# Splitting GpSimd's multiply by the reciprocals in the last attention block into two halves, one unit apart

## The chip, the cores and the metric

The kernel runs on one core of a Trainium2 chip, in one launch for all four batch images. The metric is the device time of one execution in microseconds, as the median of several runs; lower is better. The engines are named as in the profile: PE (TensorE, matrix products), PEld (its weight loads), DVE (VectorE), ACT (ScalarE), POOL (GpSimd) and SP (SyncE, which only issues transfers here).

## The reference

Layer 0 is self-attention over the 4096 positions of each 256-channel image; layer 1 normalizes, clusters, and applies an MLP and a pointwise layer to its output. The change is in layer 0:

```python
q = jnp.einsum('oc,bcn->bno', wq, xf) + bq
k = jnp.einsum('oc,bcn->bon', wk, xf) + bk[None, :, None]
attn = jax.nn.softmax(jnp.einsum('bnd,bdm->bnm', q, k), axis=-1)
v = jnp.einsum('oc,bcn->bon', wv, xf) + bv[None, :, None]
out = jnp.einsum('bcn,bmn->bcm', v, attn).reshape(B, Cc, H, W)
return gamma[0] * out + x
```

The kernel divides by the softmax denominator last: it sums the exponentials of a query's row, multiplies V by the raw exponentials, scales that by gamma, and multiplies the result by the reciprocal of the sum. That last multiply is what the change touches.

## The kernel before, in words

*Tiles and units.* An image has 8 blocks of 512 queries (`NBLK`), and each block goes over 8 groups of 512 keys (`GRP`). One group of one block is a unit, `u`; there are 64 a batch, and `nb, g = divmod(u, GRP)`. Block 7 (units 56 to 63) is the last block; in it `more` is false, since no further block has to be scored.

*One unit.* The scores of a unit lie in a tile `s` as four quarters (`B11`, `B12`, `B21`, `B22`: two halves of the keys by two halves of the queries). `exps(u + 1)`, called at the start of unit `u`, subtracts the row maximum on DVE (L655) and takes the exponentials on ACT (L659 to L661). `factors(u + 1)`, called in the middle of unit `u`, makes the sums that a seven-product scheme for 2 x 2 blocks needs: one on DVE (L678, `t13`), then four on GpSimd through `plus` (L664): `s[B12]`, `t4`, and the two running sums of the denominators, `acc` ("one" and "both"). `weigh` (L716 to L740) then issues the seven products of exponentials and V on TensorE, in four parts; the order of the products is `ORDER` = (1, 5), (2, 3), (7, 6), (4,), and in unit 63 `LAST` = (1, 5), (7, 6), (2, 3), (4,). Product 6 reads GpSimd's `s[B12]` (in the trace "av<-s,sum" behind "av<-t,sum"), product 4 reads its `t4` ("av<-t,v" in fourth place).

*What is left of the block ahead.* While block `nb` runs, block `nb - 1` is finished: `combined` (L771 to L780) puts the seven products' banks together on GpSimd, two pieces a unit in units g = 0 to 2; `total` (L782 to L795) makes the reciprocals of its denominators in a tile `rdens`; `leave(nb - 1)` (L801 to L806) multiplies the tile `t` (128 partitions, four rows of 256) by them on GpSimd, in place; `sent(nb - 1)` (L808 to L812) writes `t` to a DRAM tile `att`, as two transfers on SP's queue, one for rows 0 and 3 and one for rows 1 and 2. In block 7 `leave` stands at g = 3 (unit 59) ahead of the fourth part of `weigh`, and `sent` at g = 4 (unit 60).

*What comes after.* At unit 62 (`units - 2`) `back_one` (L832 to L835) issues on GpSimd's queue a transfer that adds block 6 of `att` to the input image `x` in SBUF; it waits until `att` is written. The `factors` of unit 63 stand behind it on GpSimd. DVE then takes block 6's statistics from that sum (`seen`, L850, and `pooled`, L855). In unit 63 the last denominators are summed on DVE (L684, L685, L748, L750), and behind the loop block 7 is finished by DVE (L779, L780, L1120, L846), while TensorE is given fills: projections of the next batch (L443), or in the last batch one block of the batch ahead (L1554). Then the cluster stage begins (L307 on). Behind `sent` SP's queue holds, from `tail` (L965 to L980): the mix weights (L167), the next image (L109) and the MLP weights (L242, L243).

*The order of work* is written out by hand: each engine runs its instructions in the order in which the program issues them, and waits on semaphores for the others. Nothing is moved by a scheduler.

Of the kernel before, what the change touches and what calls it, by code (L numbers as in the profile page):

```python
# [11 lines left out]
ALU = mybir.AluOpType  # L12
# [48 lines left out]
def attention_then_cluster_block(  # L61
# [17 lines left out]
    nc = tc.nc  # L79
# [51 lines left out]
    x00, part = load_x(0, 0, 2)  # L131
# [206 lines left out]
    def attention(b, xs, ys):  # L338
# [5 lines left out]
        qs, ks, slots, mxs, accs, tops, rdens, ts = {}, {}, {}, {}, {}, {}, {}, {}  # L344
# [452 lines left out]
        def over(nb):  # L797
            rden = rdens[nb].rearrange("p (h n) -> p h n", h=2).unsqueeze(2)
            return rden.to_broadcast([P, 2, 2, QW])

        def leave(nb):  # L801

            t = ts[nb].rearrange("p (h k) n -> p h k n", h=2)
            nc.gpsimd.tensor_tensor(t, t, over(nb), ALU.mult)
            if "t" not in own:
                own["t"] = dram.tile([NBLK // 2, P, KC, 2, NB], F32, tag="t", name=f"att_{b}")  # L806

        def sent(nb):  # L808

            t = ts.pop(nb)  # L810
            for k in range(KC):
                nc.sync.dma_start(out=own["t"][nb // 2][:, k, nb % 2], in_=rows_of(t, k))  # L812
# [126 lines left out]
        for u in range(units):  # L939
            three = u in (1, 3, 7, 9)  # L940
            for part in (0, 1, 3) if three else (0, 2) if u else (1, 3):
                if todo:
                    p, h = todo.pop(0)
# [14 lines left out]
        def weighting(next_x, fill, early, begin):  # L958

            mb, av, den, peak, quarters = None, None, iter(()), iter(()), iter(())  # L960

            views = {units - 6 + i: i for i in range(6)}
            shifts = {units - 10: 0, units - 9: 1, units - 8: 2, units - 7: 3}

            def tail(u):  # L965


                for at_u, f in (
                    (units - 12, lambda: load(0)),
                    (units - 10, lambda: (load(2), back(0))),  # L970
                    (units - 9, lambda: (load(3), back(1))),
                    (units - 8, lambda: back(2)),
                    (units - 5, lambda: (next_x(), next_x())),
                    (units - 4, lambda: (load_mix(b), next_x())),
                    (units - 4, lambda: b == B - 1 and load_mlp(b)),
                    (units - 3, lambda: (next_x(), begin())),
                    (units - 2, lambda: b < B - 1 and load_mlp(b)),
                ):
                    if u == at_u:
                        f()  # L980

            for u in range(units):
                nb, g = divmod(u, GRP)
                more = nb + 1 < NBLK
                ripe = more and nb and g == 5

                short = nb == 0 and g == 6
                if g == 0:
                    av = [
                        pool.tile([P, NB], F32, tag=tag, name=f"av{c}_{b}_{nb}")  # L990
                        for c, (pool, tag) in enumerate(
                            ((ps_a, "a0"), (ps_a, "a1"), (ps_m, "m"), (ps_m, "m"))
                        )
                    ]
                maxima = due(u, 0)
                if more and nb and g == GRP - 2:
                    next(peak)
                    if u == units - 10:
                        load(1)
                    sent(nb - 1)  # L1000
                if g == GRP - 1 and more:
                    gather(nb)
                if g + 1 < GRP or more:
                    exps(u + 1)
                for f in maxima:
                    f()
                if nb < 2 or g == 6:
                    caught(1)


                when = 1 if nb > 1 else 3
                if nb and g == when:
                    den = total(nb - 1)
                    next(den)
                elif nb and g == when + 1:
                    next(den)
                elif ripe:
                    peak = highest(nb + 1)
                    next(peak)
                if early and nb > 1:  # L1020
                    early.pop(0)()
                if u == 4:
                    spare()
                if u in views:
                    pooled(views[u])
                    seen(views[u], (0,))
                if g == GRP - 1 and not more:
                    gather(nb)
                weigh(u, av, 0)
                if short:  # L1030
                    two = ps_s.tile([P, 2, NB], F32, tag="s", name=f"tt_{b}_{nb + 1}")
                    tp = turned_over(nb + 1, two[:, 0].rearrange("p (j n) -> p j n", j=4))
                for f in due(u, 1):
                    f()
                weigh(u, av, 1)
                if short:
                    dgs["dg"] = across(nb + 1, "w2", tp)
                if u == units - 2:
                    back_one(NBLK - 2)
                maxima = due(u, 2)  # L1040
                if g == GRP - 1:
                    evict(nb, av, 0)
                    evict(nb, av, 2 if more else 1)
                if g + 1 < GRP or more:
                    factors(u + 1)
                if more and nb and g == GRP - 2:
                    known(mb)
                for f in maxima:
                    f()
                if ripe:  # L1050
                    next(peak)
                    mb = next(peak)
                if (u, 0) not in at or (u, 1) in at:
                    caught(1)
                if u in views:
                    seen(views[u], (1,))
                weigh(u, av, 2)
                if g == GRP - 1:
                    evict(nb, av, 1 if more else 2)
                if short:  # L1060
                    spread(nb + 1, dgs["dg"])
                for f in due(u, 3):
                    f()
                if nb and g == when:
                    next(den)
                elif nb and g == (5 if nb == 1 else 4 if more else 3):
                    leave(nb - 1)
                elif nb and g == 4 and not more:
                    sent(nb - 1)
                weigh(u, av, 3)  # L1070
                if g == 3 and nb + 2 < NBLK:
                    q_block(nb + 2)
                if g == GRP - 1:
                    evict(nb, av, 3)
                    quarters = combined(nb, nc.gpsimd if more else nc.vector)
                elif nb and g < 3:
                    for _ in range(2):
                        next(quarters)
                if u in shifts:
                    shift(shifts[u])  # L1080
                tail(u)

            nb = NBLK - 1
            for _ in range(4):
                next(quarters)
            if b == B - 1:
                for _ in turn_mlp():
                    pass
            table(AF.Sqrt)
            ends = b == B - 1  # L1090
            fill(1 if ends else 2)
            two = ps_s.tile([P, 2, NB], F32, tag="s", name=f"den_{b}_{nb}")
            den, inv = two[:, 0], two[:, 1]
            for j in range(4):
                nc.tensor.matmul(
                    den[j * D : (j + 1) * D, :P],
                    ones[:, :D],
                    rdens[nb][:, j * P : (j + 1) * P],
                    start=True,
                    stop=True,  # L1100
                )
            fill(1)
            rec = work.tile([P, P], F32, tag="top", bufs=1, name=f"rec_{b}_{nb}")
            nc.vector.reciprocal(rec, den[:, :P])
            for _ in quarters:
                pass
            seen(nb - 1)
            pooled(nb - 1)
            for j in range(4):
                nc.tensor.matmul(  # L1110
                    inv[:, j * P : (j + 1) * P],
                    ident[:, j * D : j * D + 1].to_broadcast([P, P]),
                    rec,
                    start=True,
                    stop=True,
                )
            nc.scalar.copy(rdens[nb], inv)
            fill(6 if ends else 7)
            t = ts[nb].rearrange("p (h k) n -> p h k n", h=2)
            nc.vector.tensor_tensor(t, t, over(nb), ALU.mult)  # L1120
            add_one(nb)
            seen(nb)
            return stats, cells, lambda: pooled(nb)
# [1042 lines left out]
```

## Time and profile before

| | us |
|---|---|
| median of 3 runs | 3116.73 |
| runs | 3112.5, 3117.52, 3116.73 |
| profiled execution | 3112.69 |
| its span, first to last instruction | 3110.9 |
| busy: PE / DVE / POOL / ACT | 3042.2 / 2501.5 / 2327.7 / 1779.4 |
| L804, the multiply: 28 instructions | 66.2 in all, 2.363 each |
| L664, GpSimd's acc, 128x512: 408 instructions | 541.4 in all, 1.347 each |
| PE waiting for POOL's s (L664) at L734, 9 times | 3.5 in all |
| granted TensorE clock | 0.998 of full speed |

How to read it: an engine's busy time counts its instructions; a share of the whole span is an average over stages with different limits, so what a change in one block is worth has to be read in that block. In the lines of the timeline the columns are start in us from the beginning of the span, duration in us, engine, line, operation, output and inputs, shapes, and, in brackets, idle time of the engine just ahead of the instruction and what ended it. "x2" is two instructions merged into one row. There are 28 L804 in four batches, one for each of the first seven blocks; the last of each batch, in block 7, starts at 501.16, 1269.19, 2036.64 and 2779.43 us.

### The profile page before, as it was taken

How to read it: one execution, taken by the hardware profiler on the slowest of the kernel's cores; microseconds unless marked ns; L12 is line 12 of the kernel's file. 1: busy time of each engine (PE TensorE's matmuls, PEld its weight loads, DVE VectorE, ACT ScalarE, POOL GpSimd, SP SyncE). 2: the span in 40 equal slices, each digit the busy share in tenths (PEclk: the TensorE clock that was granted, in tenths of full speed). 3: DMA queues.
4: the chain of work that ended last, by engine and by line, in shares of the span. 5: the costliest groups of instructions: out<-in, count | busy, mean ns of one | idle time of the engine just before them, and what ended most of it. 6: DMA issues, size and time to landing. Idle time of an engine off the chain costs nothing.

```text
span 3110.9 us, 41355 instructions
## 1 busy us (share of the span) xinstructions
PE 3042.2 (98%) x14210; PEld 2488.0 (80%) x14210; DVE 2501.5 (80%) x3548; ACT 1779.4 (57%) x2817; POOL 2327.7 (75%) x2243
## 2 busy tenths in 40 slices
PE   8999999999999999999999999999999999999999
PEld 5788887788688888878868888887877888885886
DVE  4998888777798888877779888877768988887675
ACT  5666664544566666454456666645456666655444
POOL 6888887477588888648758888965766988894563
PEclk9999999999999999999999999999999999999999
DMA  5112226100112113510011222441011212150000
GB/s 175 45 58 65 62 84 176 58 18 28 52 45 68 55 62 108 159 48 28 18 58 45 69 62 65 117 147 35 28 41 48 59 54 68 55 154 2 13 21 28
DMA packets 105570, 200.40 MB, mean 64 GB/s; under 512 B 14880, under 2 KB 30864, under 8 KB 103824
## 3 DMA queue, kind: packets, MB, share of 16 engines
q1 hardware_dynamic: 100464, 178.66, 18.0%
q0 software_dynamic: 4256, 18.90, 2.9%
q8 instruction: 113, 1.85, 0.2%
q14 instruction: 97, 0.79, 0.1%
q10 hardware_dynamic: 640, 0.20, 0.0%
HBM read 147.01 MB, written 48.34 MB: 63 GB/s over the span
## 4 chain that ended last, share of the span: by engine, by line
PE 74%; DVE 9%; POOL 8%; issue 3%; ACT 3%; DMA 2%; SPq 1%; POOLq 0%; ACTq 0%; DVEq 0%
PE av L734 34%; PE mo L1776 10%; PE sc L489 7%; PE hq L1859 5%; PE hp L1859 3%; PE hr L1859 3%; PE fv L1334 3%; POOL acc L664 3%; DVE s L655 2%; POOL t L664 2%; DVE top L513 2%; PE vp L443 1%; POOL s L664 1%; PE mo L1760 1%; DMA w<-in_w 1%
## 5 line engine op out<-in xcount | busy, mean ns | idle before, releaser
L502 ACT COPY s<-sc 128x1024 f32<-128x1024 f32 x512 | 515.1, 1012 | 427.5 <-PE sc L489 419.0
L655 DVE TENSOR_TENSOR s<-s,hold 128x1024 f32<-128x1024 f32 x512 | 598.4, 1209 | 10.7 <-ACT hold L638 5.5
L664 POOL TENSOR_TENSOR acc<-acc,t 128x512 f32<-128x512 f32 x408 | 541.4, 1347 | 0.0
L734 PE MATMUL av<-s,sum 128*128 128x256 f32 x2048 | 526.9, 380 | 3.7 <-POOL s L664 3.5
L734 PE MATMUL av<-t,v 128*128 128x256 f32 x2048 | 527.1, 380 | 2.4 <-POOL t L664 2.2
L734 PE MATMUL av<-s,v 128*128 128x256 f32 x2048 | 525.7, 379 | 2.2 <-ACT xn L1727 1.1
L664 POOL TENSOR_TENSOR s<-t,s 128x512 f32<-128x512 f32 x256 | 340.5, 1330 | 226.3 <-DVE t L678 158.9
L678 DVE TENSOR_TENSOR t<-s,hold 128x1024 f32<-128x1024 f32 x256 | 311.7, 1218 | 189.8 <-POOL acc L664 93.3
L513 DVE TENSOR_TENSOR top<-sc,top 128x1024 f32<-128x1024 f32 x350 | 426.6, 1219 | 21.6 <-ACT s L502 18.0
L734 PEld LDWEIGHTS av<-s,v 128*128 128x128 f32 x2048 | 387.2, 189 | 64.6 <-ACT xn L1727 2.3
L734 PEld LDWEIGHTS av<-t,v 128*128 128x128 f32 x2048 | 387.5, 190 | 63.1 <-POOL t L664 8.4
L734 PEld LDWEIGHTS av<-s,sum 128*128 128x128 f32 x2048 | 387.9, 190 | 61.1 <-POOL s L664 8.6
L1814 ACT ACTIVATE hs<-hs,pv_s 128x256 f32<-128x256 f32 x496 | 232.6, 503 | 352.3 <-DVE hs L1850 352.3
L489 PE MATMUL sc<-q,k 128*128 128x512 f32 x1024 | 391.6, 466 | 22.2 <-ACT s L502 10.5
L1776 PE MATMUL mo<-hs,w 128*128 128x256 f32 x1512 | 384.9, 381 | 0.0
L664 POOL TENSOR_TENSOR t<-s 128x512 f32<-128x512 f32 x256 | 329.8, 1288 | 45.4 <-PE av L734 31.9
L1776 PEld LDWEIGHTS mo<-hs,w 128*128 128x128 f32 x1512 | 283.6, 190 | 47.2 <-ACT hs L1814 6.3
L659 ACT ACTIVATE hold<-s 128x512 f32<-128x512 f32 x256 | 154.2, 602 | 214.4 <-DVE s L655 214.2
L1850 DVE TENSOR_TENSOR hs<-hq,hs 128x256 f32<-128x256 f32 x496 | 198.5, 421 | 85.8 <-PE hq L1859 75.5
L661 ACT ACTIVATE s<-s 128x1024 f32<-128x1024 f32 x256 | 266.9, 1043 | 0.0
L489 PEld LDWEIGHTS sc<-q,k 128*128 128x128 f32 x1024 | 173.7, 189 | 110.9 <-DVE top L513 59.1
L734 PE MATMUL av<-t,sum 128*128 128x256 f32 x1024 | 262.4, 378 | 0.0
(292 smaller groups left out, 4844.2 us busy)
## 6 DMA issues: line engine op xcount, KB each, us to landing
k<-k SPq DMA_DIRECT2D x248, 256.0 KB, 2.7
x<-in_x SPq DMA_DIRECT2D x62, 512.0 KB, 6.8
out<-xn SPq DMA_DIRECT2D x62, 256.0 KB, 2.1
att<-t SPq DMA_DIRECT2D x56, 256.0 KB, 4.0
x<-att POOLq DMA_DIRECT2D x12, 1024.0 KB, 9.7
w<-in_w SPq DMA_DIRECT2D x8, 1024.0 KB, 11.4
q<-q SPq DMA_DIRECT2D x31, 256.0 KB, 4.1
rden<-row_rd SPq DMA_DIRECT2D x28, 256.0 KB, 3.7
```

What stands on the lines that cost most here:

```text
L489: nc.tensor.matmul(sc[:, r, :], k_s[:, (2 * h + r) * P : (2 * h + r + 1) * P], qs[u // GRP], start=True, stop=True,)
L502: nc.scalar.copy(slots[u][:, PAIR[h]].rearrange("p h r n -> p r h n"), tiles(sc))
L513: nc.vector.tensor_tensor(top, src, top if saved[nb] is None else saved[nb], ALU.max)
L655: nc.vector.tensor_tensor(sh, sh, mb.to_broadcast([P, 2, 2, QW]), ALU.subtract)
L661: nc.scalar.activation(s[:, PAIR[1]], s[:, PAIR[1]], AF.Exp)
L664: nc.gpsimd.tensor_tensor(out, x, y, op)
L678: nc.vector.tensor_tensor(t31[u], s[:, B11 : B22 + 1 : 2], b12.to_broadcast([P, 2, 2, QW]), ALU.add)
L734: nc.tensor.matmul(av[bank][:, half_ * QW : (half_ + 1) * QW], a[:, r], t[:, r], start=(g == 0 and r == 0 and i in (1, 7, 2, 4)), stop=(g ...
L1776: return nc.tensor.matmul(bank[:, half * HB : (half + 1) * HB], a[:, j], t, start=start, stop=stop)
L1814: nc.scalar.activation(src, src, AF.Gelu_apprx_tanh, bias=pvc("b1", P, j + 4 * (i > 1)))
L1850: nc.vector.tensor_tensor(dst, ps, term, ALU.add)
L1859: nc.tensor.matmul(out, w, x, start=True, stop=True)
```

## The change

`leave` gets an argument that picks one of the two halves of `t` (rows 0 and 1, or rows 2 and 3) and of the reciprocals. Outside the last block it is called for both halves at once, as before. In block 7 it is called for the first half at g = 3 and for the second half at g = 4, just ahead of `sent`. So in each batch one GpSimd instruction on 128x1024 becomes two on 128x512, with the factors of unit 61 between them.

```diff
-        def leave(nb):
+        def leave(nb, part=slice(2)):
 
-            t = ts[nb].rearrange("p (h k) n -> p h k n", h=2)
-            nc.gpsimd.tensor_tensor(t, t, over(nb), ALU.mult)
+            t = ts[nb].rearrange("p (h k) n -> p h k n", h=2)[:, part]
+            nc.gpsimd.tensor_tensor(t, t, over(nb)[:, part], ALU.mult)
...
                 elif nb and g == (5 if nb == 1 else 4 if more else 3):
-                    leave(nb - 1)
+                    leave(nb - 1, slice(2 if more else 1))
                 elif nb and g == 4 and not more:
+                    leave(nb - 1, slice(1, 2))
                     sent(nb - 1)
```

## The prediction

> **What bounds the kernel now.** I read the page first, then the stretch around the changed line on every engine. The page's chain that ended last is 74% TensorE; GpSimd (POOL) has 8% of it. One line in that chain is the multiply that the change splits, so the question is local: does GpSimd set the pace where L804 stands in the last attention block, and what follows it?
>
> The table by stretches, for the last block of each of the four batches (from the last idle time of GpSimd ahead of it to its last product; columns: stretch, its length, busy time of PE, PEld, DVE, ACT, POOL):
>
> ```profile
> 474.87:517.62 42.75, 41.28 (x186) 34.19 (x185) 38.23 (x41) 16.81 (x27) 42.04 (x36) 1.00 0.76 214
> 1242.90:1285.60 42.70, 41.47 (x186) 34.55 (x185) 38.96 (x42) 17.56 (x27) 41.91 (x36) 1.00 0.79 221
> ```
>
> GpSimd is busy 42.04 of 42.75 us, more than TensorE. Here GpSimd is the pace-maker, which its 75% over the whole span doesn't show. The timeline of GpSimd in batch 0 (start, duration, line):
>
> ```profile
> 498.69 2.50 POOL L664 TENSOR_TENSOR acc<-acc,t 128x512 f32<-128x512 f32 x2
> 501.16 2.36 POOL L804 TENSOR_TENSOR t<-t,rden 128x1024 f32<-128x1024 f32 x1
> 503.49 1.26 POOL L664 TENSOR_TENSOR s<-t,s 128x512 f32<-128x512 f32 x1
> 504.83 1.26 POOL L664 TENSOR_TENSOR t<-s 128x512 f32<-128x512 f32 x1
> 506.05 2.50 POOL L664 TENSOR_TENSOR acc<-acc,t 128x512 f32<-128x512 f32 x2
> 508.52 1.27 POOL L664 TENSOR_TENSOR s<-t,s 128x512 f32<-128x512 f32 x1
> ...
> 513.53 1.10 POOL L833 DMA_DIRECT2D x<-att  x1
> 514.33 1.60 POOL L664 TENSOR_TENSOR s<-t,s 128x512 f32<-128x512 f32 x1
> 516.01 1.61 POOL L664 TENSOR_TENSOR t<-s 128x512 f32<-128x512 f32 x1
> 517.92 0.72 POOL L775 TENSOR_TENSOR t<-t 128x256 f32<-128x256 f32 x1 [0.30 <-ACT t L764]
> ```
>
> No bracket of idle time stands between 498.69 and 517.62: every piece starts as the one ahead of it ends. The four-piece groups are the factors of one unit (s, t, two acc): units 61 (503.49), 62 (508.52) and 63, the last, at 514.33, behind the accumulating DMA L833. TensorE at the same places:
>
> ```profile
> 503.21 1.03 PE L734 MATMUL av<-t,sum 128*128 128x256 f32 x4
> 504.80 1.13 PE L734 MATMUL av<-s,sum 128*128 128x256 f32 x4 [0.57 <-POOL s L664]
> 506.14 1.13 PE L734 MATMUL av<-t,v 128*128 128x256 f32 x4 [0.21 <-POOL t L664]
> ...
> 514.88 1.03 PE L734 MATMUL av<-t,sum 128*128 128x256 f32 x4
> 515.99 1.13 PE L734 MATMUL av<-s,sum 128*128 128x256 f32 x4
> ```
>
> TensorE is held twice. In unit 61 it waits for the s and t that stand behind L804: the unit takes 499.76 to 507.11, 7.35 us, where unit 62 takes 507.11 to 513.15, 6.04 us; so L804 costs it 1.31 us there. In unit 63 its "s,sum" group starts 1.11 us after the group ahead instead of the usual 0.86: it waits 0.25 us for the s that GpSimd ends at 514.33 + 1.60 = 515.93. This second wait is the one that ends last. Batches 1 and 2 show the same two waits; in batch 3 the second is 0.52.
>
> **The change part by part.** In the order of the built program nothing moves but this, once per batch (four of the 28 L804): L804 on 128x1024 becomes L804 on 128x512 in its old place, and another 128x512 behind the factors of unit 61. The other 24 stay whole.
>
> *GpSimd time.* L804 takes 503.49 − 501.16 = 2.33 us from start to start. A 128x512 without a wait takes 2.47 / 2 = 1.235 (two acc, 498.69 to 501.16). So two halves cost 2.47: **+0.14 us** a batch. Lowest by the rows: the t group at 504.83, 1.22, gives +0.11; highest: s to t with its semaphore wait, 503.49 to 504.83, 1.34, gives +0.35. Neither half waits for the instruction ahead of it, so I take 0.14. It can't be a gain: the elements are the same. The other rate is in the Trainium skill, GPSIMD Engine Reference, section "Instruction dispatch": each instruction costs one indirect call, tens of cycles. At 1.2 GHz that is some 0.04 us by an estimate from that page, and four times that is 0.2 us instead of 0.56; the row decides.
>
> *First half.* It ends at 501.16 + 1.24 = 502.40, so unit 61's s starts 1.09 us earlier, is ready at 503.67, and t at 505.02. TensorE reaches "s,sum" of unit 61 at 503.21 + 0.86 = 504.07 without a wait, and "t,v" at 504.94, waiting some 0.1. Unit 62 starts near 506.04 instead of 507.11: −1.07 us.
>
> *Second half.* Unit 61's factors take 5.03 us (503.49 to 508.52), so it runs 507.43 to 508.67, and unit 62's s starts at 508.67 instead of 508.52. TensorE wants it at 510.35 and has it at 509.94; t is there at 511.29, wanted at 511.22. Unit 63 starts at about 512.3, against 513.15. Its DVE part (L678, 510.23 + 1.22 = 511.45) and its exps are there. It then wants s at 514.91. But L833 now starts at 513.67 and the s behind it ends at 516.07: TensorE starts "s,sum" at 516.13 against 515.99. **All that was gained in unit 61 is waited away in unit 63**, where GpSimd is late by its whole sum of work, and that sum grew by 0.14.
>
> *Behind the block.* DVE's timeline shows that it hangs on GpSimd too (wait in brackets):
>
> ```profile
> 512.40 1.74 DVE L684 TENSOR_TENSOR acc<-acc,t 128x512 f32<-128x512 f32 x1 [0.95 <-POOL acc L664]
> 514.24 2.25 DVE L685 TENSOR_TENSOR acc<-acc 128x512 f32<-128x512 f32 x1
> ```
>
> From 512.40 DVE runs without a gap to the denominators (L750) and, through L1104 and the last products, to L307 at 529.88, for which TensorE then waits 0.27 us. So 0.14 us passes on whole into the cluster stage, where the chain is TensorE's.
>
> *The queue of SyncE.* Both att writes (L812) need both halves (rows 0 and 3, rows 1 and 2), and SP issues in order:
>
> ```profile
> 503.55 0.89 SPq L812 DMA_DIRECT2D att<-t  x2
> 504.48 0.99 SPq L167 DMA_DIRECT2D mix<-in_wfv  x2
> ```
>
> They now go at 508.70 and 509.13, 5.15 us later, and all behind them too: mix (2), x of the next batch (4), w (2). Readers: mix is read at 534.2 (L1172), w at 543.7 (L251), those x later still; free. L833 waits for att in GpSimd's queue, with the factors of unit 63 behind it. In these four places att landed 2.3 to 3.4 us after its issue, so by 512.6, and L833 starts at 513.67: free, with 1.1 us to spare. L833 itself landed 8.9 us after its issue, so at 522.6; its reader is DVE's L850 at 523.79: free, 1.3 us to spare. In batch 3, w1 is also read by TensorE at 2798.37 (L1554): issued at 2788.99 instead of 2783.84, landing 7.7 us later at 2796.7: free by 1.7 us.
>
> **Sum.** 4 x 0.14 = +0.56 us. The profiled execution took 3112.69 us (span 3110.9 and 1.8 around it), so 3113.25 by it. The median of the runs is 3116.73, 4 us above the profiled one; on that the forecast is **3117.3 us**. About 0.2%, 6.2 us, is what a measurement of this kernel can tell from no change.
>
> **Rivals.**
> 1. *L833 waits for att, on the slower side.* Place: GpSimd's queue before unit 63. It decides from a landing later than 513.67 − 509.13 = 4.5 us after the second issue. For: over all 56 att writes the median is 4.0 and the longest 8.6. Against: the eight that matter took 2.3 to 3.4, and SP's queue has issued nothing for the time ahead of them. Price at 8.6: 4.1 us a batch, +16.4 and the 0.56: 3133.7. The Trainium skill, DMA: Bandwidth & Descriptors, section "Latency and other measured facts", has the latency of HBM rise from 0.2 us to 2 us at high load, which speaks for this rival; by an estimate from it 3.4 would become 5.2 and the wait 0.7 a batch. No row here shows it at these places.
> 2. *The moved loads collide.* In the 5 us later window x, mix and w are all still ahead when L833 starts. If L833 lands in 11.3 us (the longest of the 1 MB L828) instead of 8.9, DVE waits 1.0 us in batches 0 to 2; if w1 takes 12.4 us in batch 3 (as in batch 0), TensorE waits 3.0 once. Together +6.0, with 0.56: 3123.3. Against: the DMA engines were already full under L833 (DMA share 1.00 to 1.07 from 512 to 520), so its share of them shouldn't fall.
> 3. *TensorE keeps what unit 61 wins.* If s of unit 63 weren't last, 1.31 x 4 = −5.2: 3111.5. For: the waits of 0.57 and 0.21 are the largest TensorE has for GpSimd. Against: 515.99, above; GpSimd has no idle time to make this from.
> 4. *The change does nothing of the kind:* excluded, the split stands in the built order.
>
> **How the numbers follow.** Forecast 0.80, rival 1 0.06, rival 2 0.09, rival 3 0.05. The range goes from rival 3 to rival 2, 3111.5 to 3123.3, and leaves out rival 1; the forecast's own ends are 4 x 0.11 and 4 x 0.35, 3117.2 to 3118.1. Faster by over 0.2%: 0.02 (part of rival 3). Slower: 0.09 (rival 1, the far end of rival 2). Same: 0.89.
>
> **What would show it.** Two L804 of about 1.27 us, 6.3 us apart. No or little wait in unit 61; a wait of 1 us or more for POOL s in unit 63, with "s,sum" about 14.97 us after the start of the first half (now 14.83 after L804's). L833 12.5 us after that start (now 12.37), with no wait. It would be wrong if L833 starts later than that, if DVE idles ahead of L850 behind it, or if unit 63 shows no wait.

## The result and the profile after

The change made the kernel slower. The median is 3125.03 us (9 runs, 3120.1 to 3127.9), against 3115.10 for the kernel before, run beside it (9 runs, 3111.4 to 3117.5): ratio 1.0033, 95% interval 1.0025 to 1.0042. The profiled execution has a span of 3123.2 us against 3110.9, so 12.3 us more, and a granted clock of 0.996 against 0.998.

The timeline of GpSimd in the kernel after, batch 0 (start, duration, engine, line):

```profile
500.96 1.28 POOL L804 TENSOR_TENSOR t<-t,rden 128x512 f32<-128x512 f32 x1
...
507.24 1.26 POOL L804 TENSOR_TENSOR t<-t,rden 128x512 f32<-128x512 f32 x1
...
513.49 1.09 POOL L833 DMA_DIRECT2D x<-att  x1
514.29 1.58 POOL L664 TENSOR_TENSOR s<-t,s 128x512 f32<-128x512 f32 x1
```

Two halves of 1.28 and 1.26 us, 6.28 us apart, and L833 12.53 us after the first one's start, without a bracket: it doesn't wait for att. TensorE in units 61 to 63 of the same kernel:

```profile
503.88 1.03 PE L734 MATMUL av<-s,sum 128*128 128x256 f32 x4
504.86 1.13 PE L734 MATMUL av<-t,v 128*128 128x256 f32 x4
...
513.84 1.03 PE L734 MATMUL av<-t,sum 128*128 128x256 f32 x4
515.92 1.13 PE L734 MATMUL av<-s,sum 128*128 128x256 f32 x4 [1.06 <-POOL s L664]
```

The waits of 0.57 and 0.21 us in unit 61 are gone, and unit 63 waits 1.06 us for GpSimd's s, 14.96 us after the first half's start. Up to here the forecast holds. Then DVE, behind the loop:

```profile
523.40 0.41 DVE L780 TENSOR_TENSOR t<-t,t 128x256 f32<-128x256 f32 x1
525.82 1.29 DVE L850 BATCH_NORM_STATS2 st<-x 128x6 f32<-128x512 f32 x2 [2.02 <-DMA x<-att]
...
531.92 0.59 DVE L307 BATCH_NORM_AGGREGATE mv_gn<-st 128x2 f32<-128x96 f32 x1
```

L850 waits 2.02 us for L833's data. In the kernel before it started at 523.79 without a wait:

```profile
523.79 1.28 DVE L850 BATCH_NORM_STATS2 st<-x 128x6 f32<-128x512 f32 x2
```

In the kernel after the same bracket is 1.43 in batch 1, 2.22 in batch 2, and absent in batch 3. L833 now takes 12.3, 11.7, 12.5 and 8.9 us to land; before, 8.9 three times and 6.2. Its own issue is on time. TensorE behind it:

```profile
532.56 0.59 PE L309 MATMUL gnm_gn<-mv_gn,left 128*128 128x1 f32 x2 [2.37 <-DVE mv_gn L307]
533.01 0.57 PE L310 MATMUL gnm_gn<-mv_gn,avg 128*128 128x1 f32 x2
533.44 2.06 PE L443 MATMUL vp<-wv_s,x 128*128 128x256 f32 x4
535.28 0.42 PE L320 MATMUL gnv_gn<-mv_gn,avg 128*128 128x1 f32 x2
535.57 3.76 PE L443 MATMUL vp<-wv_s,x 128*128 128x256 f32 x8
```

The same two places in the kernel before:

```profile
530.52 0.38 PE L309 MATMUL gnm_gn<-mv_gn,left 128*128 128x1 f32 x2 [0.27 <-DVE mv_gn L307]
...
532.07 1.97 PE L443 MATMUL vp<-wv_s,x 128*128 128x256 f32 x8
```

The bracket ahead of L309 was 0.27 us and is 2.37. And something else has happened: the eight matmuls of L443 that took 1.97 us take 3.76. The table by stretches (stretch, its length, busy time of PE, PEld, DVE, ACT and POOL, then granted clock, DMA share and GB/s) says why:

```profile
529.50:532.50 3.00, 0.69 (x4) 0.26 (x2) 2.96 (x5) 0.58 (x1) 0.00 (x0) 0.99 0.00 0
532.50:534.00 1.50, 1.44 (x5) 1.36 (x6) 0.36 (x4) 0.00 (x0) 0.00 (x0) 0.50 0.00 0
534.00:535.60 1.60, 1.60 (x7) 1.32 (x5) 1.53 (x5) 0.00 (x0) 0.00 (x0) 0.50 0.00 0
535.60:539.10 3.50, 3.50 (x9) 2.75 (x10) 1.17 (x6) 1.56 (x3) 0.00 (x0) 0.50 0.00 0
```

From 532.46 to 539.28, 6.8 us, TensorE runs at half its clock. In the kernel before, the same work had 1.00.

**Where the 12.3 us are.** I measured from the start of L804 (the first half) to L307, and from L307 to the first matmul of the cluster stage (fv<-mix, L1334, L1335 after), in each batch:

| batch | L804 to L307, before | after | L307 to fv, before | after | sum of both: after − before |
|---|---|---|---|---|---|
| 0 | 28.72 | 30.96 | 8.75 | 11.63 | 5.12 |
| 1 | 28.70 | 30.36 | 8.75 | 9.96 | 2.87 |
| 2 | 28.71 | 31.18 | 8.75 | 8.75 | 2.47 |
| 3 | 29.56 | 29.70 | 8.17 | 9.85 | 1.82 |

The last column sums to 12.28 us, the whole difference of the spans. L307 is later by 6.51 in all, of which 5.67 is DVE's wait for L833. The time behind L307 is longer by 5.77, all of it in the three batches where the clock fell. In two of them (4.09 us) TensorE's idle ahead of L309 had grown, from 0.27 and 0.26 us to 2.37 and 1.78. In batch 3 (1.68 us) it had not: 1.91 us before, 1.92 after.

### The profile page after: what moved, and what is told of

Same layout as the page of the kernel before. It is cut to its first block, busy times and chain, and to the rows that moved or that the text cites. A ratio compares the mean times of both kernels' runs of the same rounds, so it can differ in the third digit from the quotient of the medians.

```text
span 3123.2 us, 41356 instructions
## 1 busy us (share of the span) xinstructions
PE 3048.0 (98%) x14210; PEld 2495.9 (80%) x14210; DVE 2503.8 (80%) x3548; ACT 1778.8 (57%) x2817; POOL 2327.8 (75%) x2247
## 4 chain that ended last, share of the span: by engine, by line
PE 75%; DVE 9%; POOL 7%; issue 3%; ACT 3%; DMA 2%; SPq 0%; ACTq 0%; POOLq 0%; DVEq 0%
PE av L734 35%; PE mo L1777 9%; PE sc L489 7%; PE hq L1860 5%; PE hr L1860 3%; PE hp L1860 3%; PE fv L1335 3%; POOL acc L664 2%; DVE s L655 2%; PE vp L443 2%; DVE top L513 1%; POOL t L664 1%; PE mo L1761 1%; POOL s L664 1%; DMA x<-att 1%
## 6 DMA issues: line engine op xcount, KB each, us to landing
x<-att POOLq DMA_DIRECT2D x12, 1024.0 KB, 10.1
```

## The experiments

Three theories. **A**: SP issues in order, so the late att pushed 4.4 MB of loads (mix, x, w) into the time in which L833 transfers; L833 lands late. **B** (rival): the split itself, two instructions with a unit between them, costs the time. **C**, beside A: some 5.8 us of the 12.3 are the clock, which falls after TensorE's longer idle ahead of L309. Every edit is against the changed kernel unless it says otherwise; ratios are to the kernel before, run on the same chip. The interval stands in brackets.

**e1: the loads ahead of att.**

```diff
-                    (units - 5, lambda: (next_x(), next_x())),
-                    (units - 4, lambda: (load_mix(b), next_x())),
...
+                    (units - 5, lambda: (next_x(), next_x(), load_mix(b))),
+                    (units - 5, lambda: (next_x(), next_x(), load_mlp(b))),
```

> The split stays, but SP's queue holds mix, the next image and the MLP weights ahead of the two att writes (all issued at the end of unit 59), so they no longer run beside L833. Theory A (the loads that moved 5 us later fill the DMA engines under L833, which lands late, and DVE waits for it ahead of L850): L833 lands in 8.9 us or less instead of 11.7 to 12.5, DVE has no wait at L850, TensorE no idle time over 1 us ahead of L309 in batches 0 to 2, and the time is that of before plus 4 x 0.14: 3115.7, within 0.1% of before. Theory B (the split itself costs, through GpSimd's extra instructions and the wait in unit 63): the time stays that of the change, 3125, since the halves stand where they stood.

Measured: 3137.21 us, 1.0070 [1.0057, 1.0083]. The time I expected was missed by 21 us. L833 itself landed in 6.4 to 6.8 us and L850 did not wait, as A has it. But att now stood behind the loads on SP's queue, its two writes landed 10.3 and 9.5 us after their issue in batch 0, and GpSimd waited for them:

```profile
520.39 1.11 POOL L833 DMA_DIRECT2D x<-att  x1 [6.46 <-DMA att<-t]
```

That is rival 1 of the prediction, made real by the edit: 6.46 us in batch 0, 15.9 us in three batches, with unit 63 held behind it; at each of the three the clock also fell to 0.50 for 6.8 us. It says that the order on SP's queue cuts both ways, and nothing yet on A against B.

**e2: late, but whole.** No split; L804 on 128x1024 at g = 4, ahead of `sent`.

```diff
-                    leave(nb - 1, slice(2 if more else 1))
+                    if more:
+                        leave(nb - 1)
                 elif nb and g == 4 and not more:
-                    leave(nb - 1, slice(1, 2))
+                    leave(nb - 1)
```

> No split: the whole L804 on 128x1024 stands at g = 4 of the last block, behind the factors of unit 61, where the change has its second half; att and the loads behind it go out as late as in the change. Theory A: as slow as the change, 3124 to 3126, with L833 landing in 11.7 to 12.5 us and waits of 1.4 to 2.2 us at L850 in batches 0 to 2. Theory B: that of before, 3115, since there is one instruction as before.

Measured: 3124.27 us, 1.0030 [1.0019, 1.0042]; L833 lands in 11.3 to 12.6 us in batches 0 to 2 and in 9.4 in batch 3, and L850 waits 1.8, 1.0 and 2.3 us, close to what A expected. The slowdown is there without any split.

**e3: split, but not late.** Both halves one behind the other at g = 3.

```diff
                     leave(nb - 1, slice(2 if more else 1))
+                    if not more:
+                        leave(nb - 1, slice(1, 2))
                 elif nb and g == 4 and not more:
-                    leave(nb - 1, slice(1, 2))
                     sent(nb - 1)
```

> The split alone: both halves at g = 3, one behind the other, so att and the loads go out as in before (0.14 us later). Theory A: 3115.7, within 0.1% of before; L833 lands in 8.9 us. Theory B: 3125, since both instructions are there.

Measured: 3115.35 us, 1.0000 [0.9991, 1.0009]. L833 lands in 6.6 to 9.0 us, no wait. B falls for two halves side by side.

**e5: split one unit apart, but a unit earlier**, so that att is on time.

```diff
-                    leave(nb - 1, slice(2 if more else 1))
+                    leave(nb - 1, slice(0 if more else 1, 2))
                 elif nb and g == 4 and not more:
-                    leave(nb - 1, slice(1, 2))
                     sent(nb - 1)
...
                     for _ in range(2):
                         next(quarters)
+                    if g == 2 and not more:
+                        leave(nb - 1, slice(1))
```

> Both halves one unit earlier, still one unit apart: the first in unit 58 behind the combinations L779 and L780, the second in unit 59, and att written where it was before. Nothing is left out. Theory A (the shifted loads, not the split, cost the time): SP gets past att at 503 to 505 us again, L833 lands 8.5 to 9.0 us after its issue in batches 0 to 2, DVE does not wait at L850, TensorE's idle ahead of L309 is 0.2 to 0.5 us, time 3115 to 3116.5, within 0.05% of before. The rival that halves standing one unit apart cost time by themselves on GpSimd: the L850 wait is gone and the time still stays above 3119.

Measured: 3115.25 us, 1.0002 [0.9993, 1.0011]. GpSimd and, in the second fence, DVE:

```profile
495.88 1.27 POOL L804 TENSOR_TENSOR t<-t,rden 128x512 f32<-128x512 f32 x1
...
502.15 1.28 POOL L804 TENSOR_TENSOR t<-t,rden 128x512 f32<-128x512 f32 x1
```

```profile
523.71 1.28 DVE L850 BATCH_NORM_STATS2 st<-x 128x6 f32<-128x512 f32 x2
```

Halves 6.27 us apart, as in the change, and no bracket at L850. B is refuted in this form too: what costs is the lateness of att and of what stands behind it.

**e7 and e8: what in the moved loads makes L833 late?** e7 moves the two w loads (2 MB) ahead to unit 58; e8 leaves as much behind att but puts w ahead of x.

```diff
e7:
-                    (units - 4, lambda: b == B - 1 and load_mlp(b)),
+                    (units - 6, lambda: load_mlp(b)),
...
-                    (units - 2, lambda: b < B - 1 and load_mlp(b)),
e8:
-                    (units - 4, lambda: (load_mix(b), next_x())),
-                    (units - 4, lambda: b == B - 1 and load_mlp(b)),
-                    (units - 3, lambda: (next_x(), begin())),
-                    (units - 2, lambda: b < B - 1 and load_mlp(b)),
+                    (units - 4, lambda: (load_mix(b), load_mlp(b))),
+                    (units - 3, lambda: (next_x(), next_x())),
+                    (units - 3, lambda: begin()),
```

> The change with the two w loads (2 MB) moved ahead of att, to unit 58, where SP is idle; x 2 and 3 and mix stay behind att, which stays late. So 2.4 MB instead of 4.4 MB stand behind att on SP's queue. Nothing is left out. Theory A by bytes (what is still outstanding on SP's queue when L833 starts sets its landing): some 1.3 MB outstanding as in batch 3 of the change, L833 lands 8.5 to 9.8 us after issue, DVE's wait at L850 is under 0.5 us in each batch, time 3115 to 3118. Rival by packet size (L833 shares the DMA engines with x packets of 3.7 KB instead of w packets of 1 KB): x is still beside it, so L833 lands 11 us or later, DVE waits over 1 us in batches 0 to 2, time 3121 or more.

> The change with the order behind att turned round: mix, then both w loads, then x 2 and 3. As many bytes stand behind att as in the change, but while L833 runs the first 2 MB of them are w's packets of about 1 KB. Nothing is left out. Theory A by bytes: L833 lands 11.5 to 12.5 us after issue in batches 0 to 2 as in the change, DVE waits 1.4 to 2.2 us, time 3123 to 3126. Rival by packet size: L833 lands about 9 us after issue, no wait at L850, time 3115 to 3118.

Measured: e7 3114.97 us, 1.0002 [0.9993, 1.0011], L833 lands in 10.1 to 10.3 us in batches 0 to 2; e8 3114.01 us, 1.0002 [0.9994, 1.0011], L833 lands in 9.3 to 9.7. Neither has a wait at L850. e7's landing lies between its two expectations, above bytes' 9.8 and below packets' 11. e8 is the telling one: att as late as in the change, as many bytes behind it, and the whole slowdown is gone. SP's queue and L850 in e8:

```profile
509.53 0.89 SPq L812 DMA_DIRECT2D att<-t  x2
510.46 0.98 SPq L167 DMA_DIRECT2D mix<-in_wfv  x2
511.54 0.51 SPq L242 DMA_DIRECT2D w<-in_w  x1
512.17 0.40 SPq L243 DMA_DIRECT2D w<-in_w  x1
512.67 3.89 SPq L109 DMA_DIRECT2D x<-in_x  x4
```

```profile
524.73 1.28 DVE L850 BATCH_NORM_STATS2 st<-x 128x6 f32<-128x512 f32 x2
```

So "bytes outstanding" alone doesn't set the landing. The packets show a reason. The next three fences are the queues in one microsecond while L833 transfers (q0 is GpSimd's queue with L833, q1 is SP's; packets, MB, share of the engines), all in batch 0 and each at L833's full rate: 5.5, 7.0 and 5.5 us after its issue. The kernel before, 519.03 to 520.03, with w beside:

```profile
q0 software_dynamic: 76, 0.16, 83.6%
q1 hardware_dynamic: 70, 0.08, 27.4%
```

The change, 520.49 to 521.49, with x beside:

```profile
q0 software_dynamic: 53, 0.11, 58.3%
q1 hardware_dynamic: 51, 0.18, 49.6%
```

e8, 519.98 to 520.98, with w beside again:

```profile
q0 software_dynamic: 77, 0.16, 84.7%
q1 hardware_dynamic: 76, 0.08, 29.0%
```

In each, the two queues get almost equally many packets. Beside w, whose packets are some 1.1 KB (0.08 MB / 70), L833 gets 76 of them through in a microsecond; beside x, at 3.5 KB (0.18 / 51), 53. L833 has 272 packets, so 272 / 76 = 3.6 us against 272 / 53 = 5.1: the rate makes some 1.5 of the 3.4 us between 8.9 and 12.3, by this estimate. The other 1.9 lie in its beginning, which is later and slower: in the change only 7 of its packets have moved 5.5 us after its issue, in the kernel before 70. What makes it begin so is not shown. The Trainium skill, DMA: Bandwidth & Descriptors, section "Queues, rings and completion order", states that an SDMA engine goes round robin between the queue rows it has work for, packet by packet; the rows above (76 to 70, 53 to 51, 77 to 76) agree, if the profile's packets are those that the page means.

**e10: the same, without any lateness.** The kernel before, with e8's order behind att.

> The kernel before, its product whole and in its old place, and only the order behind att turned round: mix, both w loads, then x 2 and 3. So att is on time and as many bytes stand on SP's queue when L833 starts as in the kernel before, but the packets beside L833's own are now x's of 3.7 KB and no longer w's of 1 KB. Nothing is left out. By packet size: beside x L833 gets about 50 packets a microsecond instead of 75 to 80, starts a little later and lands 10.3 to 12 us after issue in batches 0 to 2 instead of 8.9, DVE waits at L850 for 0 to 1.7 us a batch, time 3115 to 3121, and the wait comes back with no lateness at all. By bytes outstanding: 8.5 to 9.2 us, no wait, time 3114 to 3116.

Measured: 3114.09 us, 1.0000 [0.9991, 1.0010]; L833 lands in 9.6 to 9.9 us in batches 0 to 2, no wait at L850. Between the two expectations: the landing grew by 0.8 us beside x, with 54 packets of its own to 51 of SP's in the full microsecond 519.34 to 520.34, but x had mostly run out 6.5 us after L833's issue, and then L833 sped up to 75 packets a microsecond. e7 shows the same, with 89 at the end. So the rate follows what stands beside L833 at the time: x to the end in the change, for part of it in e7 and e10, hardly in e8 and before. Alone (e1) it gets up to 100.

**e4 and e9: the clock.** e4 gives TensorE more of the fill ahead of L309, e9 gives it 11 matmuls whose result nobody reads.

```diff
e4:
-            fill(6 if ends else 7)
+            fill(6 if ends else 9)
e9:
             fill(6 if ends else 7)
+            for _ in range(11):
+                nc.tensor.matmul(
+                    den[:, :P], ident, ident, start=True, stop=True
+                )
```

> The change, with two more units of projections (1.9 us of TensorE work) issued ahead of the group norm in batches 0 to 2 (fill of 9 instead of 7), so that TensorE isn't idle while DVE waits for L833. L833 stays late (11.7 to 12.5 us) and DVE's waits of 1.4 to 2.2 us stay. Theory C (of the 12.3 us by which the profiled span grew, about 5.8 come from the granted clock, which falls to 0.5 after TensorE's longer idle time): the idle time ahead of L309 falls to 0.7 us or less, the clock stays at 1.00 there in batches 0 and 1, and the time falls by 3 to 4 us from the change, to 3121. Without C (the clock falls for another reason): 3125 as the change, with the clock falling at the same places.

Measured: 3144.46 us, 1.0091 [1.0078, 1.0105]. In batch 0 the clock stayed at 1.00 behind L309, but the longer fill put key projections into the path of the group norm (new waits of TensorE ahead of pcen, the next product of the cluster stage, 7.3 us in three batches, and 9.4 us in four places for L1673), and in batches 1 and 2 the clock fell 7 and 9 us behind L309. The idle ahead of L309 was 0.6 us or less, as expected, but the 3121 us was missed by 23, so it tells nothing on C.

> The change with 11 matmuls of ident by ident, 128x128, added behind the fill ahead of L309: about 1.6 us of TensorE work a batch whose result nobody reads, and which is shorter than the idle of 1.78 to 2.58 us there, so it delays nothing. The output's computation is whole. Theory C (5.8 of the 12.3 us are the granted clock falling after this idle): L833 and DVE's waits of 5.7 us in 3 batches stay as in the change, the clock stays 1.00 behind L309 in all four batches, time 3118 to 3120. Rival (the clock falls for another reason, or costs nothing on the path): the time stays 3124 to 3126.

Measured: 3119.92 us, 1.0019 [1.0010, 1.0028]. The timeline of TensorE in batch 0, and the clock behind it:

```profile
529.00 2.62 PE L1121 MATMUL den<-ident 128*128 128x128 f32 x22
531.45 0.28 PE L309 MATMUL gnm_gn<-mv_gn,left 128*128 128x1 f32 x2
```

```profile
531.40:534.40 3.00, 3.00 (x19) 2.74 (x19) 2.23 (x8) 0.61 (x2) 0.00 (x0) 1.00 0.00 0
534.40:537.90 3.50, 3.23 (x23) 2.22 (x25) 2.48 (x9) 2.41 (x5) 0.00 (x0) 1.00 0.02 5
```

The added work took 2.45 us and not the 1.6 that I had put down, so it was no cover for free: L309 starts 0.25 to 0.89 us later behind L307 than in the kernel before. In spite of that, and of 4.1 us of DVE waits that are still there (5.7 in the change's profile), the time fell: the clock held 1.00 behind L309 in all four batches.

**e11 and e12: change and e9 on one chip.** The two medians above come from different chips, so both ran again together.

> The change itself once more, as the partner of the next kernel on one chip. Nothing is left out. Theory A with C: 1.0025 to 1.0042 of the kernel before, as measured the first time, DVE's waits at L850 5 to 6 us in 3 batches, the clock at 0.5 behind L309 in at least one batch.

> The change with the 11 added matmuls a batch whose result nobody reads, as before, now beside the change on the same chip. Theory C: 3 to 6 us below the change on this chip, with the clock at 1.00 behind L309 in all four batches and DVE's waits at L850 still 4 us or more. Rival (the two medians so far differed by their chips): within 1.5 us of the change.

Measured: the change 3123.46 us (6 runs), 1.0028 [1.0017, 1.0040], with waits at L850 of 4.1 us in three batches, less than expected; e12 3120.24 us (11 runs), 1.0018 [1.0009, 1.0027], with 3.2, less than the 4 expected. The difference is 3.2 us, near C's lower end. In e11's profile the clock fell behind L309 in all four batches (idle 1.69, 1.49, 2.03 and 1.91 us), and L307 to fv took 10.03, 10.03, 10.04 and 9.85: 5.5 us more in all than before. In e12 it fell in none. e12 takes 37.0 us for the same four stretches against 39.95, although with the added matmuls L309 starts 3.0 us later behind L307 in all.

That filling the idle keeps the clock up is shown: the clock fell behind L309 in seven of the eight batches of the change's two profiles, and in none of the eight of e9 and e12. What this is worth in the median is less sure. The 3.2 us hold some 0.9 us of shorter waits, have the cost of the added matmuls against them, and the single runs overlap (3119.2 to 3126.9 and 3119.4 to 3122.9). Within the six runs of the change the time goes with the clock: 3119.2, 3121.4 and 3121.7 us at a mean of 0.997 to 0.998, 3125.2 to 3126.9 at 0.994 to 0.996. The means of the two groups are 3120.8 and 3125.9, so the same kernel differs by some 5 us from run to run; which sets which these figures alone don't say.

## Why the prediction was wrong

*GpSimd as pace-maker: right.* Halves of 1.27 us, 6.28 apart; L833 12.53 us after the first's start (forecast 12.5). e8 shows the forecast almost alone: fv comes 37.63, 37.59, 37.59 and 37.84 us after the first half, against 37.47, 37.45, 37.46 and 37.73, so +0.16, +0.14, +0.13 and +0.11. The sum was to be 4 x 0.14 = 0.56 and is 0.54.

*The gain of unit 61 is waited away in unit 63: right*, 14.96 us after the first half against 14.97 forecast; rival 3 falls with it.

*L833 doesn't wait for att: right.* The att writes landed 2.3 to 3.5 us after their issue, and no bracket stands at L833. Rival 1 came only in e1, where loads stood ahead of att.

*w1 in batch 3, mix, x and w: right.* No wait for any of them appears.

*"L833 itself landed 8.9 us after its issue, so at 522.6; its reader is DVE's L850 at 523.79: free, 1.3 us to spare": this step failed.* The 8.9 was taken over from the profile before, although the step ahead of it had just moved 4.4 MB on another queue 5.15 us later, further into this transfer. It became 11.7 to 12.5 in batches 0 to 2; 1.3 us were spent and 1.4 to 2.2 more were waited. In batch 3, without x, the landing went from 6.2 to 8.9 and stayed free.

*Rival 2 named this mechanism and place* and put 11.3 us and 3123.3 on it, with a chance of 0.09. What I held against it, that "the DMA engines were already full under L833, so its share of them shouldn't fall", was the wrong inference: the two queues got about equally many packets (53 to 51), so L833's share fell from 83.6% to 58.3% beside packets three times as large, and it also began later. The view to ask was the queues in a window of a microsecond, not the DMA share. The time was 1.7 us past rival 2 and outside the range. The base of the forecast, 3116.73, was itself 1.6 us high: counted from 3115.10, the change cost 9.9 us, where the forecast had 0.56 and rival 2 had 6.6.

*A term was missing: the clock.* Neither forecast nor rival priced what an idle of some 2 us ahead of L309 can do to the matmuls behind it. The fallen clock gave 5.77 of the 12.28 us in the profiled execution: 4.09 behind idles that L833's lateness had opened, and 1.68 in batch 3, where the idle was no longer than before and the fall seems a matter of when it came (last section). As far as the traces show, that part is chance.

## What to carry to other kernels

When an edit delays one transfer on a queue that issues in order, everything behind it moves too: list what it will now overlap, and don't take a landing time over from the old overlap. A small transfer on one queue was slowed by large packets on another (53 a microsecond against 76), so here the urgent one did better with the small packets beside it (e8), and an urgent write must not stand behind bulk loads on its own queue (e1). A wait that opens an idle on TensorE costs more than its length where the clock falls behind it.

None of these versions beats the kernel before: e3, e5, e7, e8 and e10 have ratios of 1.0000 to 1.0002.

## What the runs showed of the hardware that was not expected

- The granted clock fell to 0.50 behind idles of 1.49 to 2.69 us ahead of L309 (2.69 in e2, batch 2). The Trainium skill, TensorE: Matmul & The Clock Gate, section "Why this matters for your kernels", advises no idle gaps above some 3 us between bursts; here shorter ones were enough, and the measurement decides.
- The length of the idle alone doesn't decide: 2.58 us (change, batch 2) was followed by no fall, and 1.91 or 1.92 in batch 3 by none in the kernel before, e1, e3, e4, e5, e7 and e8, and by one in the change, e10 and e11. The page's section "What's actually happening" has the window free-running, so the phase would matter. The traces fit that: in every profile all changes of the clock lie on one grid with steps of 3.41 us (in the change 532.46, 539.28, 1307.28, 1310.69 and so on). In the change's batches 0, 1 and 3 one step held 2.26, 1.42 and 1.43 us of the idle, and the clock fell at its end; in batch 2 the 2.58 us lay in two steps, 1.29 in each, and in batch 3 of the kernel before 1.31 and 0.60. Over all profiles no step with up to 1.38 us of this idle was followed by a fall, and every step with 1.42 us or more was, but for three in batch 3 (1.67 in e1, 1.88 in e4, 1.92 in e8), which ended within 0.25 us of L309's start. No run moved the phase on purpose, and what sets these three apart stays open.
- L833's first packet moved 1.8 us after its issue with nothing beside it (e1) and 4.3 to 5.3 us after it beside SP's loads. The size of their packets doesn't set this: 5.5 us after issue in batch 0 some 70 packets had moved in the kernel before and in e8, about 60 in e10, where x stood beside it, and 10 or fewer in e7, e2 and the change. Why it begins later in these was not tried.
- In batches 0 to 2 the delay of L307 is 0.22 to 0.25 us more than L850's wait, of which 0.14 is GpSimd's. Most of the other 0.1 lies in how the bracket counts: without a wait L850 starts 0.33 us after L780 (523.46 and 523.79 in the kernel before), a little ahead of L780's end, and the bracket counts from that end.
